# Disjoint segments in the STU's second products, and sums over states issued for two units together

## The chip, the cores and the metric

The kernel runs on one core of one Trainium2 chip. The metric is the device time of one execution in microseconds. All data is fp32.

## The reference

The input is four images of 48 × 48 tokens with 128 channels. Two layers are computed, one after the other, for each image.

The first is a state-space layer: projections, a 3 × 3 convolution, and a recurrence over the 2304 tokens in four directions k, for 256 channels with 16 states each:

```python
def step(h, inp):
    dt_l, u_l, B_l, C_l = inp
    dA = jnp.exp(dt_l[..., None] * A)
    h = h * dA + (dt_l * u_l)[..., None] * B_l[:, :, None, :]
    y = jnp.einsum('bkdn,bkn->bkd', h, C_l)
    return (h, y)
```

The second is an attention without projections, and after it an STU: a causal convolution of the sequence with 16 spectral filters, once plain (U_plus) and once with alternating signs (U_minus), and a product with a matrix for each filter, plus an autoregressive part over three shifted copies of the sequence:

There are four such STUs with their own matrices; the i-th reads only the first T, T/2, T/4 or T/8 tokens, and their results are added with four weights:

```python
out = jnp.einsum('btkd,k,kde->bte', U_plus, s, Mpp)
out = out + jnp.einsum('btkd,k,kde->bte', U_minus, s, Mpm)
...
for i, frac in enumerate((1, 2, 4, 8)):
    si = _stu(x[:, :T // frac], sigma, phi, M_u[i], M_phi_plus[i], M_phi_minus[i])
...
return jnp.sum(stacked * weights, axis=-1)
```

As the convolution is causal and the same for all four, a token's convolved rows are multiplied by one matrix: the weighted sum of the matrices of those STUs that reach the token. There are four such sums, with boundaries at tokens 288, 576 and 1152.

## The kernel before

**Stages.** For each image there is a scan stage (the recurrence), then an epilogue with the attention. The STU of an image is the filler of the next image's scan stage: `stu` is a generator that issues a few matmuls at a time, and `scans` calls it through `more(share)`, which pulls filler until the matmul columns issued so far (`done[0]`) reach the given share of all columns of the stage. In scan stage 0 the filler is `mixture`, which makes the mixed matrices G of the STU. The STU of the fourth image runs alone at the end. All loads and stores of these parts are issued by SP in program order; PE, VectorE (DVE), ScalarE (ACT) and GpSimd (POOL) each work through their own order, which is written out by hand.

**The scan.** A chunk is one direction and 384 tokens; a stage has 24 chunks. Of each chunk there are eight units (h, q), two halves of the channels by four groups of four states. Step s of `scans` deals with several units at once: `enter` multiplies the input for units s + 1 and s + 2 into a tile `s` (L457, five of eight units on DVE, three on POOL), `scan` runs unit s in four parts (L464 exponential on ACT, L467 scan on DVE), `times_c` multiplies unit s - 1 by C on POOL (L475, L476), `spread` makes the row B of unit s + 2 on PE (L448), and `sum_c` adds up the states of unit s - 2 on PE (L484): four matmuls with a 128 × 32 stationary matrix, each into its own 32 partitions of the bank `y`. After the fourth unit of a half, `add_y` adds the bank to the output on DVE (L490), one step later. The tiles `s` come from a pool of six buffers, the bank `y` from a pool of one.

**The STU.** Four tokens make a row, so that a sequence has 576 rows; `BLOCKS` cuts them into blocks (lo, hi, place, extra). For each block and each of 16 filters k, `conv` issues six groups of convolution matmuls (L990), with the filter's loaded windows `tt` (L960, four buffers) as moving operand; ACT and DVE take their results into U (L1004, L1016, L1019); and `project` multiplies U by the mixed matrices G (L1056) into the bank `p` (shown as `pr` in the profile) that is kept for the whole block. Once a block, `ar` adds the autoregressive products (L1046). In the first three blocks the sum of matrices changes after 72, 16 and 32 rows (rows 72, 144 and 288 of the sequence). There the kernel multiplies all rows by the matrix that holds after the boundary, and then the first `extra` rows once more by the difference to the one that holds before it:

```python
return ((w, 1), (extra, 0)) if extra else ((w, 0),)
```

So G and the autoregressive matrices are stored with six places: three differences and three accumulated mixtures. `mixture` makes them in two groups of matmuls (L847) for each filter and half, in two banks, and ACT copies each (L822).

Of the kernel before, what the change touches and what calls it, by code (L numbers as in the profile page):

```python
# [8 lines left out]
F32 = mybir.dt.float32  # L9
AF = mybir.ActivationFunctionType  # L10
ALU = mybir.AluOpType
# [4 lines left out]
P = 128  # L16
# [5 lines left out]
CS = 384  # L22
# [3 lines left out]
KF = 16  # L26
# [7 lines left out]
SLOT = 2 * (LF + 1)  # L34


BLOCKS = [(0, 128, 0, 72), (128, 256, 2, 16), (256, 384, 4, 32), (384, 512, 5, 0), (512, 576, 5, 0)]
SHIFT = 55.0


# [14 lines left out]
def hybrid_kernel(ctx: ExitStack, tc: tile.TileContext, a: dict, out: bass.AP):  # L55
# [80 lines left out]
    zs = res.tile([NH, P, L], F32, name="zd")  # L136
    td = res.tile([L, C], F32, name="td")
    ud = res.tile([P, 4, 1 + LF], F32, name="ud")
    gd = res.tile([KF, P, 2, 2 * NF - 2, C], F32, name="gd")
    mud = res.tile([P, 2 * NF - 2, 3, C], F32, name="mud")  # L140
    fd = res.tile([KF, 3, 2, LF + P], F32, name="fd")
    xdd = [[res.tile([P, CS], F32, name=f"xdd{k}_{c}") for c in range(L // CS)] for k in range(2)]

# [374 lines left out]
    def scans(b, chunks, preps, front, sp, back, work, work_cols):  # L518

        units = [Unit(ch, h, q) for ch in chunks for h, q in quads]  # L520
        total = len(chunks) * CHUNK_COLS + work_cols
        done = [0]

        def more(share):

            while done[0] < share * total:
                cols = next(work, None)
                if cols is None:
                    break
                done[0] += cols  # L530

        def enter(s):

            if s + 2 < len(units) and units[s + 2].pool:
                units[s + 2].enter(sp.s)
            if 0 <= s + 1 < len(units) and not units[s + 1].pool:
                units[s + 1].enter(sp.s)

        def spread(s):
            if s < len(units) and not units[s].pool:  # L540
                units[s].spread(back.psB)
                done[0] += CS

        def prepare(s):

            ci, j = divmod(s, len(quads))
            for c in range(ci + 1, ci + 4):
                if c < len(chunks) and 0 <= s - len(quads) * c + LEAD < STEPS:
                    done[0] += next(preps[c]) or 0

        def refill(s, i):

            if 0 <= s < len(units) and s // len(quads) + 1 < len(chunks):
                u, nxt = units[s], chunks[s // len(quads) + 1]
                if u.h == NH - 1:
                    nxt.fetch(i + u.q, front)

        pending = []
        dAs = [back.psa.tile([P, 512], F32, tag=f"dA{i}", name=f"dA{b}_{i}") for i in range(2)]
        for t in dAs:  # L560
            nc.vector.memset(t[:, 0:CS + 2:CS + 1], 0.0)
        spread(0)
        enter(-2)
        enter(-1)
        spread(1)
        for s in range(len(units) + 2):
            real = s < len(units)
            enter(s)
            prepare(s)
            if real:  # L570
                units[s].scan(0, dAs)
            more((s + 0.25) / len(units))
            if 1 <= s <= len(units):
                units[s - 1].times_c()
            if real:
                units[s].scan(1, dAs)
            if pending:
                pending.pop().add_y()
            prepare(s)
            more((s + 0.5) / len(units))  # L580
            spread(s + 2)
            if real:
                units[s].scan(2, dAs)
            more((s + 0.75) / len(units))
            prepare(s)
            if real:
                units[s].scan(3, dAs)
            refill(s - 3, Q4)
            if s + 1 < len(units) and units[s + 1].pool:
                refill(s + 1, 0)  # L590
            if s >= 2:
                units[s - 2].sum_c(back.psy)
                done[0] += CS
                if units[s - 2].q == Q4 - 1:
                    pending.append(units[s - 2])
            more((s + 1) / len(units))
        for u in pending:
            u.add_y()
        assert next(work, None) is None
# [141 lines left out]

    MIX_COLS = KF * 2 * 2 * (6 + 3) * C

    ws = wp.tile([P, KF, NF], F32, name="ws")

    def weights(one):
# [48 lines left out]
        quarter = one.tile([P, KF], F32, name="quarter")  # L797
        nc.vector.memset(quarter, 0.25)
        nc.gpsimd.tensor_tensor(sg, sg, quarter, ALU.pow)
        mum = one.tile([P, 2 * NF - 2, 3, C], F32, name="mum")  # L800
        nc.vector.tensor_scalar_mul(mum[:, 5], mu[:, 0], wts[:, 0:1])
        for i in range(1, NF):
            nc.vector.tensor_scalar_mul(mum[:, 6 - 2 * i], mu[:, i], wts[:, i:i + 1])
            if i < NF - 1:
                nc.vector.tensor_tensor(mum[:, 5 - 2 * i], mum[:, 7 - 2 * i], mum[:, 6 - 2 * i], ALU.add)
            yield
        nc.scalar.dma_start(mud, mum)
        for i in range(NF):
# [5 lines left out]
    def mixture(pool, ps):  # L814

        late = []
        banks = [0]

        def keep_(G, p, j, k, q):
            nc.scalar.copy(G[:, :, j], p)  # L822
            if j == 0:
                nc.sync.dma_start(gd[k, :, q], G.rearrange("p s j c -> p (s j) c"))

        for k in range(KF):
            M = [pool.two.tile([P, NF, C], F32, tag=f"M{j}", name=f"M{j}_{k}") for j in range(2)]
            for t, src in zip(M, ("M_phi_plus", "M_phi_minus")):
                nc.sync.dma_start(t, a[src][:, k].rearrange("i d e -> d i e"))

            W = pool.two.tile([P, 2, NF, P], F32, tag="W", name=f"W{k}")
            for i in range(NF):
                nc.scalar.activation(W[:, 0, i], ident, AF.Copy, scale=ws[:, k, i:i + 1])
                nc.scalar.activation(W[:, 1, i], nident, AF.Copy, scale=ws[:, k, i:i + 1])
            yield 0
            for q in range(2):
                G = pool.two.tile([P, 3, 2, C], F32, tag="Gm", name=f"Gm{k}_{q}")
                for j in (1, 0):
                    p = ps.psc.tile([P, 3, C], F32, tag=("c", "q0", "q1")[banks[0] % 3], name=f"G{k}_{q}_{j}")
                    banks[0] += 1  # L840
                    for i in range(NF):

                        n = NF - 1 - i if j else 1
                        if i == (NF - 1 if j else 0):
                            continue
                        for t in range(2):
                            nc.tensor.matmul(p[:, :n] if j else p[:, NF - 1 - i], W[:, q if t else 0, i],  # L847
                                             M[t][:, i].unsqueeze(1).to_broadcast([P, n, C]) if j else M[t][:, i],
                                             start=(t == 0 and (i == 0 or not j)),
                                             stop=(t == 1 and (i == NF - 2 or not j)))  # L850
                            yield n * C
                    if late:
                        keep_(*late.pop())
                    late.append((G, p, j, k, q))
        keep_(*late.pop())

    def begin_stu(b):
# [6 lines left out]
    def tail(b, J, T, po, pool, ps):  # L864
# [38 lines left out]
        for j in range(4):  # L903
# [5 lines left out]
        nc.sync.dma_start(ud[:, :, 1 + P * J:1 + P * J + k], uT.rearrange("c (j p) -> c j p", j=4))  # L909

    STU_COLS = sum(KF * 12 * sum(hi - max(lo, J * P) for J in range((hi + P - 1) // P))
                   + (2 * KF + 3) * 4 * (hi - lo + extra) + 4 * (hi - lo) for lo, hi, place, extra in BLOCKS)

    def stu(b, pool, ps):

# [116 lines left out]

        def parts(w, extra):

            return ((w, 1), (extra, 0)) if extra else ((w, 0),)

        def ar(n):

            (lo, hi, place, extra), k = items[n]
            w = hi - lo  # L1040
            p = ps.psp.tile([P, 512], F32, tag="p", name=f"pr{b}_{n}")
            now["p"] = p = p[:, :4 * w].rearrange("p (f r m) -> p f r m", f=2, r=2)
            for i, (v, x) in enumerate(parts(w, extra)):
                for j in range(3):
                    src = now["x"][:, 2 - j:6 - j].rearrange("p (r f) m -> p f r m", f=2)
                    nc.tensor.matmul(p[:, :, :, :v], now["mu"][:, x, j, :], src[:, :, :, :v],  # L1046
                                     start=(i == 0 and j == 0), stop=False)
            yield 3 * 4 * (w + extra)

        def project(n):  # L1050
            (lo, hi, place, extra), k = items[n]
            w = hi - lo
            p = now["p"].rearrange("p f r m -> p (f r) m")
            for q in range(2):
                for v, x in reversed(parts(w, extra)):
                    nc.tensor.matmul(p[:, :, :v], Gs[n][:, q, x, :], U[n][:, 4 * q:4 * q + 4, :v], start=False,  # L1056
                                     stop=(k == KF - 1 and q == 1 and v == w))
                yield 4 * (w + extra)
            if k == KF - 1:
                late.append(lambda: kept(n, now["p"], w))  # L1060

# [192 lines left out]
```

## Time and profile before

| | us |
|---|---|
| median of 3 runs (6332.32 to 6337.62) | 6336.3 |
| the profiled execution | 6347.6 |
| its span, first to last instruction | 6345.8 |
| PE busy | 5413.9 |
| DVE busy | 4482.4 |
| POOL busy | 3637.0 |
| ACT busy | 3050.9 |
| scan stage 0, first to last scan | 123.9 to 1136.7 |
| scan stages 1, 2 and 3 | 1439.0 to 2556.4, 2858.8 to 3976.8, 4278.8 to 5390.3 |
| the last STU alone | 5637 to 6345.8 |

Busy time is the time in which an engine has at least one instruction in work; for PE it is modelled. The profile comes from one execution, which took 11.3 us more than the median of the runs. In the profile each fp32 matmul appears as two records, so that counts of PE are twice those of the code. DMA share is the mean busy share of the core's 16 DMA engines.

### The profile page before, as it was taken

To read this page: it belongs to the slowest core of one execution; us is meant where nothing else is said; L and a number is where in the kernel's file an instruction comes from. 1 tells how busy PE (TensorE), PEld (TensorE's weight loads), DVE (VectorE), ACT (ScalarE), POOL (GpSimd) and SP (SyncE) were. 2 spreads that over 40 slices of the span, in tenths; PEclk is the share of its full clock that TensorE was granted. 3 is DMA by queue.
4 is the path that set the end of the run, shared out by engine and by line. 5 is a ranking of instruction groups with operands and counts; after the bars stand their busy time and mean duration, and the time that the engine had idled before them with its cause. 6 is when DMAs were issued, how large, how long until landed. Compare 5 with 4: busy or idle time off the path is not lost.

```text
span 6345.8 us, 76244 instructions
## 1 busy us (share of the span) xinstructions
PE 5413.9 (85%) x25032; PEld 3360.4 (53%) x25032; DVE 4482.4 (71%) x5562; ACT 3050.9 (48%) x6461; POOL 3637.0 (57%) x1825
## 2 busy tenths in 40 slices
PE   3665666788999998788999998789999998889999
PEld 1222222444555666534556667534555666557889
DVE  6998899458888997458889987458899987211000
ACT  2666666245555654245556654246566654222111
POOL 1888888306787886207778886207778877100000
PEclk6777787799999999899999999889999999899999
DMA  4656655127788888127788888127888887025446
GB/s 105 145 139 150 154 144 143 35 64 180 193 213 218 228 220 237 40 63 188 194 208 223 226 229 223 37 71 189 197 213 221 226 224 222 20 74 153 149 142 214
DMA packets 658251, 1033.57 MB, mean 163 GB/s; under 512 B 93856, under 2 KB 515872, under 8 KB 633120
## 3 DMA queue, kind: packets, MB, share of 16 engines
q1 hardware_dynamic: 652032, 1025.00, 62.7%
q10 hardware_dynamic: 5824, 3.69, 0.3%
q8 instruction: 200, 3.28, 0.2%
q14 instruction: 195, 1.60, 0.1%
HBM read 905.79 MB, written 122.56 MB: 162 GB/s over the span
## 4 chain that ended last, share of the span: by engine, by line
PE 50%; DMA 19%; DVE 18%; ACT 4%; SPq 3%; issue 3%; POOL 3%; DVEq 0%; ACTq 0%; POOLq 0%
PE cv L990 23%; DMA tt<-fd 8%; DVE s L467 7%; PE pr L1056 7%; DMA rep<-dtdud 6%; PE y L484 4%; DVE s L457 4%; PE s L726 3%; PE o L719 3%; DMA bc<-xdd 2%; PE B L448 2%; PE op L662 2%; DVE xc L266 2%; DMA G<-gd 2%; POOL s L476 2%
## 5 line engine op out<-in xcount | busy, mean ns | idle before, releaser
L467 DVE TENSOR_TENSOR_SCAN s<-dA,s 128x385 f32<-128x385 f32 x3072 | 2760.2, 942 | 382.8 <-ACT dA L464 379.6
L476 POOL TENSOR_TENSOR s<-s,bc 128x1536 f32<-128x1536 f32 x768 | 2439.0, 3177 | 200.7 <-DVE s L467 104.3
L464 ACT ACTIVATE dA<-rep,A 128x384 f32<-128x384 f32 x3072 | 1781.9, 585 | 1259.9 <-DVE s L467 1219.1
L990 PE MATMUL cv<-tt,u 128*128 128x256 f32 (+3 forms) x7680 | 1650.8, 354 | 129.2 <-DMA tt<-fd 65.5
L990 PEld LDWEIGHTS cv<-tt,u 128*128 128x128 f32 x7680 | 1271.9, 193 | 649.1 <-issue 303.9
L457 POOL TENSOR_TENSOR s<-rep,bc 128x1536 f32<-128x1536 f32 x288 | 994.0, 3451 | 92.9 <-DMA bc<-xdd 92.9
L457 DVE TENSOR_TENSOR s<-rep,B 128x1536 f32<-128x1536 f32 x480 | 832.8, 1735 | 83.3 <-PE B L448 54.1
L990 PE MATMUL cv<-tt,us 128*128 128x256 f32 (+3 forms) x3840 | 855.2, 352 | 37.2 <-DMA tt<-fd 31.3
L484 PE MATMUL y<-s,csum 128*32 128x384 f32 x6144 | 717.3, 542 | 115.1 <-DVE ya L490 78.8
L990 PEld LDWEIGHTS cv<-tt,us 128*128 128x128 f32 x3840 | 640.7, 192 | 231.5 <-issue 64.7
L1019 DVE TENSOR_TENSOR U<-cv,Q 128x256 f32<-128x256 f32 (+1 forms) x640 | 244.5, 382 | 705.5 <-PE cv L990 696.9
L1056 PE MATMUL pr<-U,G 128*128 128x512 f32 (+4 forms) x2048 | 693.2, 468 | 2.1 <-ACT U L1016 2.1
L448 PE MATMUL B<-xd,spread 128*128 128x384 f32 x960 | 440.1, 543 | 175.5 <-DVE s L457 166.7
L1016 ACT COPY U<-cv 128x256 f32<-128x256 f32 (+1 forms) x640 | 223.0, 349 | 700.9 <-PE cv L990 700.3
L475 POOL COPY carry<-s 128x4 f32<-128x4 f32 x640 | 120.7, 189 | 691.3 <-DVE s L467 660.0
L1056 PEld LDWEIGHTS pr<-U,G 128*128 128x128 f32 x2048 | 335.8, 190 | 193.6 <-issue 140.7
L1004 ACT COPY Q<-cv 128x256 f32<-128x256 f32 (+3 forms) x640 | 223.0, 349 | 385.2 <-PE cv L990 381.7
L726 PE MATMUL s<-xnT 128*128 128x512 f32 (+1 forms) x720 | 357.7, 582 | 42.6 <-ACT xnT L688 23.4
L728 ACT ACTIVATE e<-s,shift 128x512 f32<-128x512 f32 (+1 forms) x360 | 231.0, 644 | 314.1 <-PE s L726 313.5
L484 PEld LDWEIGHTS y<-s,csum 128*32 128x32 f32 x6144 | 127.1, 112 | 467.0 <-issue 314.0
L160 POOL TENSOR_TENSOR ln_vu<-ln_vu,mhalf 128x4 f32<-128x4 f32 (+1 forms) x20 | 26.8, 1340 | 601.9 <-DVE ln_vu L159 601.9
L719 PE MATMUL o<-e,xn 128*128 128x512 f32 (+1 forms) x720 | 343.2, 560 | 4.5 <-ACT e L728 4.5
(161 smaller groups left out, 3761.9 us busy)
## 6 DMA issues: line engine op xcount, KB each, us to landing
rep<-dtdud SPq DMA_DIRECT2D x768, 384.0 KB, 7.7
tt<-fd SPq DMA_DIRECT2D x192, 577.0 KB, 5.3
bc<-xdd SPq DMA_DIRECT2D x2304, 48.0 KB, 3.5
tt<-fd SPq DMA_DIRECT2D x192, 513.0 KB, 4.6
tt<-fd SPq DMA_DIRECT2D x192, 385.0 KB, 4.3
dtdud<-re SPq DMA_DIRECT2D x768, 96.0 KB, 2.3
G<-gd SPq DMA_DIRECT2D x192, 256.0 KB, 5.6
tt<-fd SPq DMA_DIRECT2D x64, 514.0 KB, 5.9
```

Of the source, the lines that this page charges most:

```text
L448: nc.tensor.matmul(self.bt[:, :CS], spread[:, self.ch.k // 2, self.q].rearrange("p c j -> p (c j)"), self.ch.xd, start=True, stop=True)
L457: eng.tensor_tensor(s, self.ch.rep[self.h][:, 1], bt.unsqueeze(1).to_broadcast([P, G4, CS]), ALU.mult)
L464: nc.scalar.activation(dA[:, 1:CS + 1], ch.rep[self.h][:, 0, g], AF.Exp, scale=A[:, ch.k, self.h * G4 + g, self.q:self.q + 1])
L467: nc.vector.tensor_tensor_scan(s, dA[:, CS + 1:0:-1] if ch.rev else dA[:, :CS + 1], s, 0.0, ALU.mult, ALU.add)
L476: nc.gpsimd.tensor_tensor(self.s, self.s, ch.bc[Q4 + self.q].unsqueeze(1).to_broadcast([P, G4, CS]), ALU.mult)
L484: nc.tensor.matmul(ch.y[g * DL:(g + 1) * DL, :CS], csum, self.s[:, g], start=(self.q == 0), stop=(self.q == Q4 - 1))
L719: nc.tensor.matmul(po[J][:, :w], xn[:, i], e[:, :w], start=(i == 0), stop=(i == NT - 1))
L726: nc.tensor.matmul(p[:, :w], xnT[:, i * P:(i + 1) * P], xnT[:, 512 * J:512 * J + w], start=True, stop=True)
L728: nc.scalar.activation(e[:, :w], p[:, :w], AF.Exp, bias=shift)
L990: nc.tensor.matmul(p2[:, :, at - first:], x, t[:, :, hi - 1 - at + J * P:end if end >= 0 else None:-1], start=(c < 2 and J == 0), stop=(J ...
L1019: nc.vector.tensor_tensor(dst, src, q, ALU.add)
L1056: nc.tensor.matmul(p[:, :, :v], Gs[n][:, q, x, :], U[n][:, 4 * q:4 * q + 4, :v], start=False, stop=(k == KF - 1 and q == 1 and v == w))
```

## The change

Two things change. In the STU, the rows before a boundary are multiplied by their own accumulated mixture and the rows after it by theirs: two disjoint segments of the bank in place of all rows and a correction. The mixture then has four places in place of six, made in one group of matmuls into one bank for each filter and half, with one copy and a smaller store. In the scan, the sums over states of units s - 3 and s - 2 are issued together at every second step, where before those of unit s - 2 were issued at each step. The counts of columns by which the filler is paced follow.

```diff
-BLOCKS = [(0, 128, 0, 72), (128, 256, 2, 16), (256, 384, 4, 32), (384, 512, 5, 0), (512, 576, 5, 0)]
+BLOCKS = [(0, 128, 0, 72), (128, 256, 1, 16), (256, 384, 2, 32), (384, 512, 3, 0), (512, 576, 3, 0)]
...
-    gd = res.tile([KF, P, 2, 2 * NF - 2, C], F32, name="gd")
-    mud = res.tile([P, 2 * NF - 2, 3, C], F32, name="mud")
+    gd = res.tile([KF, P, 2, NF, C], F32, name="gd")
+    mud = res.tile([P, NF, 3, C], F32, name="mud")
...
-            if s >= 2:
+            if s >= 2 and units[s - 2].q % 2:
+                units[s - 3].sum_c(back.psy)
                 units[s - 2].sum_c(back.psy)
-                done[0] += CS
+                done[0] += 2 * CS
                 if units[s - 2].q == Q4 - 1:
                     pending.append(units[s - 2])
...
-    MIX_COLS = KF * 2 * 2 * (6 + 3) * C
+    MIX_COLS = KF * 2 * NF * (NF + 1) * C
...
         for i in range(1, NF):
-            nc.vector.tensor_scalar_mul(mum[:, 6 - 2 * i], mu[:, i], wts[:, i:i + 1])
-            if i < NF - 1:
-                nc.vector.tensor_tensor(mum[:, 5 - 2 * i], mum[:, 7 - 2 * i], mum[:, 6 - 2 * i], ALU.add)
+            nc.vector.tensor_scalar_mul(mum[:, NF - 1 - i], mu[:, i], wts[:, i:i + 1])
+            nc.vector.tensor_tensor(mum[:, NF - 1 - i], mum[:, NF - 1 - i], mum[:, NF - i], ALU.add)
...
-        def keep_(G, p, j, k, q):
-            nc.scalar.copy(G[:, :, j], p)
-            if j == 0:
-                nc.sync.dma_start(gd[k, :, q], G.rearrange("p s j c -> p (s j) c"))
+        def keep_(p, k, q):
+            G = pool.two.tile([P, NF, C], F32, tag="Gm", name=f"Gm{k}_{q}")
+            nc.scalar.copy(G, p)
+            nc.sync.dma_start(gd[k, :, q], G)
...
-                for j in (1, 0):
-                    p = ps.psc.tile([P, 3, C], F32, tag=("c", "q0", "q1")[banks[0] % 3], name=f"G{k}_{q}_{j}")
...
+                p = ps.psc.tile([P, NF, C], F32, tag=("c", "q0", "q1")[banks[0] % 3], name=f"G{k}_{q}")
+                banks[0] += 1
+                for i in range(NF):
+
+                    n = NF - i
+                    for t in range(2):
+                        nc.tensor.matmul(p[:, :n], W[:, q if t else 0, i],
+                                         M[t][:, i].unsqueeze(1).to_broadcast([P, n, C]),
+                                         start=(t == 0 and i == 0), stop=(t == 1 and i == NF - 1))
+                        yield n * C
...
-                   + (2 * KF + 3) * 4 * (hi - lo + extra) + 4 * (hi - lo) for lo, hi, place, extra in BLOCKS)
+                   + (2 * KF + 3) * 4 * (hi - lo) + 4 * (hi - lo) for lo, hi, place, extra in BLOCKS)
...
-            return ((w, 1), (extra, 0)) if extra else ((w, 0),)
+            return ((0, extra, 0), (extra, w, 1)) if extra else ((0, w, 0),)
...
-            for i, (v, x) in enumerate(parts(w, extra)):
+            for v0, v1, x in parts(w, extra):
                 for j in range(3):
                     src = now["x"][:, 2 - j:6 - j].rearrange("p (r f) m -> p f r m", f=2)
-                    nc.tensor.matmul(p[:, :, :, :v], now["mu"][:, x, j, :], src[:, :, :, :v],
-                                     start=(i == 0 and j == 0), stop=False)
-            yield 3 * 4 * (w + extra)
+                    nc.tensor.matmul(p[:, :, :, v0:v1], now["mu"][:, x, j, :], src[:, :, :, v0:v1],
+                                     start=(j == 0 and v0 == 0), stop=False)
+            yield 3 * 4 * w
...
             for q in range(2):
-                for v, x in reversed(parts(w, extra)):
-                    nc.tensor.matmul(p[:, :, :v], Gs[n][:, q, x, :], U[n][:, 4 * q:4 * q + 4, :v], start=False,
-                                     stop=(k == KF - 1 and q == 1 and v == w))
-                yield 4 * (w + extra)
+                for v0, v1, x in parts(w, extra):
+                    nc.tensor.matmul(p[:, :, v0:v1], Gs[n][:, q, x, :], U[n][:, 4 * q:4 * q + 4, v0:v1], start=False,
+                                     stop=(k == KF - 1 and q == 1 and v1 == w))
+                yield 4 * w
```

More of the change, by code (lines that the diff above doesn't have):

```diff
@@ L799, in weights @@
         nc.gpsimd.tensor_tensor(sg, sg, quarter, ALU.pow)
-        mum = one.tile([P, 2 * NF - 2, 3, C], F32, name="mum")
-        nc.vector.tensor_scalar_mul(mum[:, 5], mu[:, 0], wts[:, 0:1])
+        mum = one.tile([P, NF, 3, C], F32, name="mum")
+        nc.vector.tensor_scalar_mul(mum[:, NF - 1], mu[:, 0], wts[:, 0:1])
         for i in range(1, NF):
-            nc.vector.tensor_scalar_mul(mum[:, 6 - 2 * i], mu[:, i], wts[:, i:i + 1])
-            if i < NF - 1:
-                nc.vector.tensor_tensor(mum[:, 5 - 2 * i], mum[:, 7 - 2 * i], mum[:, 6 - 2 * i], ALU.add)
+            nc.vector.tensor_scalar_mul(mum[:, NF - 1 - i], mu[:, i], wts[:, i:i + 1])
+            nc.vector.tensor_tensor(mum[:, NF - 1 - i], mum[:, NF - 1 - i], mum[:, NF - i], ALU.add)
             yield
@@ L836, in mixture @@
             for q in range(2):
-                G = pool.two.tile([P, 3, 2, C], F32, tag="Gm", name=f"Gm{k}_{q}")
-                for j in (1, 0):
-                    p = ps.psc.tile([P, 3, C], F32, tag=("c", "q0", "q1")[banks[0] % 3], name=f"G{k}_{q}_{j}")
[L840 to L854, printed above, removed]
+                p = ps.psc.tile([P, NF, C], F32, tag=("c", "q0", "q1")[banks[0] % 3], name=f"G{k}_{q}")
[7 more added lines that the diff above has]
+                        yield n * C
+                if late:
+                    keep_(*late.pop())
+                late.append((p, k, q))
         keep_(*late.pop())
```

## The prediction

> **What bounds the kernel now.** I read the slices of the page first. They fall into four scan stages, an attention stage after each, and a last stage in which the STU of the fourth image runs alone. Then I cut the span into windows. The first row below is scan stage 0 (with the weight mixture as filler), the next three are thirds of scan stage 2 (with the STU of image 1 as filler), the last is the lone STU. Columns: microseconds, busy time with instruction counts of the named engines, granted clock, DMA share, GB/s.
>
> ```profile
> core 0: us, PE busy (x) PEld busy (x) DVE busy (x) ACT busy (x) POOL busy (x), PEclk, DMA share, GB/s
> 149.00:1090.00 941.00, 580.78 (x2533) 234.89 (x2532) 855.86 (x917) 583.41 (x1195) 812.98 (x399) 0.78 0.61 147
> 2860.00:3310.00 450.00, 416.94 (x1850) 240.50 (x1851) 385.14 (x457) 264.05 (x580) 341.46 (x168) 0.97 0.80 196
> 3310.00:3760.00 450.00, 438.99 (x2143) 278.16 (x2143) 419.00 (x483) 273.91 (x578) 380.69 (x183) 1.00 0.88 224
> 3760.00:3965.00 205.00, 178.19 (x1293) 140.51 (x1292) 159.71 (x190) 98.17 (x232) 144.85 (x70) 0.94 0.83 230
> 5637.00:6345.80 708.80, 698.82 (x3460) 568.28 (x3460) 67.09 (x165) 115.14 (x325) 0.00 (x0) 0.99 0.54 161
> ```
>
> The lone STU is PE and nothing else (699 of 709 us). Stage 0 is the scan's DVE (91%), and PE has 360 us to spare. Stages 1 to 3 look alike: PE leads at 93% to 98%, DVE follows at 86% to 93%, DMA at 0.80 to 0.88. The chain of waits, asked for a stretch of the middle third and then of the last third, says which holds where:
>
> ```profile
> by line: PE cv L990 61.1%; PE y L484 14.4%; PE pr L1056 10.7%; PE B L448 6.9%; PE dt L386 3.4%; issue 1.9%; DVE s L467 1.8%; DVE s L457 0.1%
> ...
> by line: DMA tt<-fd 36.3%; PE cv L990 35.9%; PE y L484 6.8%; DVE s L467 4.4%; PE B L448 3.7%; DVE s L457 3.5%; PE pr L1056 3.0%; PE dt L386 1.4%; DMA bc<-xdd 1.3%; DVE re L414 0.8%; issue 0.8%; PE pr L1046 0.7%; DVE U L1019 0.4%; PE ot L107
> ```
>
> From 3560 to 3660 us it is a PE chain; from 3770 to 3960 us (the 64-row block) the filter loads take over a third. For the prices I read PE's timeline. Each fp32 matmul is two records, so the sum of one unit over states, four matmuls, is "x8".
>
> ```profile
> 3309.46 0.60 PE L990 MATMUL cv<-tt,us 128*128 128x258 f32 x2
> 3309.99 0.85 PE L484 MATMUL y<-s,csum 128*32 128x384 f32 x8
> 3310.77 1.13 PE L990 MATMUL cv<-tt,us 128*128 128x258 f32 x4
> 3311.74 1.24 PE L1056 MATMUL pr<-U,G 128*128 128x128 f32 x4
> ...
> 3318.99 0.81 PE L448 MATMUL B<-xd,spread 128*128 128x384 f32 x2
> 3319.63 0.59 PE L990 MATMUL cv<-tt,u 128*128 128x256 f32 x2
> ...
> 5663.85 2.85 PE L1056 MATMUL pr<-U,G 128*128 128x288 f32 x8
> 5666.53 1.47 PE L990 MATMUL cv<-tt,u 128*128 128x256 f32 x6
> ```
>
> Durations of PE overlap, so starts are what counts. From start to start a 256-column record takes 0.216 us, 384 columns 0.32 (the B row: 0.64 for two), 288 columns 0.242, 512 columns 0.429, so 0.83 ns a column. The pr row checks it: 4 × 0.429 + 4 × 0.242 = 2.68 = 5666.53 - 5663.85. Around y the rule breaks. Two cv records take 0.53 instead of 0.43 before it, y takes 0.78 instead of 0.65 (two rounds of four concurrent column groups), the four cv records after it 0.97 instead of 0.87. The medians over all y groups of stages 1 to 3 are 0.093 + 0.129 + 0.107 = **0.33 us lost for each y group**.
>
> **What the skill says.** TensorEngine Tiling (Array Packing), Key Properties: changing the tiling mode drains TensorE, and tiles of one mode run independently. The trace agrees: the 0.33 us stand where 128*128 and 128*32 meet, the four y records of a round start 7 ns apart, and where two units follow each other at the end of stage 1 (2552.24 us) their rounds start at 0, 0.35, 0.67, 0.99 us, with nothing lost between units. PSUM — Partial Sum Buffer, Specifications, says that a non-contiguous access pattern slows matmuls much, which would hit the 56-column segments that the change brings. The trace disagrees: the existing segments of 4 × 72 columns take 0.242 us, what 288 contiguous columns would. DMA: Bandwidth & Descriptors, Issuing engines are not separate DMA queues: all share 16 engines; the last third, with 230 GB/s and the tt chain, fits that.
>
> **The change, part by part.** *Second products (L1056).* Per half q a block with a boundary had one full-width product and one of 4 × extra columns; now it has 4 × extra and 4 × (w - extra). The count stays, two matmuls of two records. Block 0 loses 288 columns (429 to 189 ns a record), block 1 64 (429 to 375), block 2 128 (429 to 323): 2 × (240 + 54 + 106) = 800 ns per half, × 2 halves × 16 filters = 25.6 us per image. *Autoregressive products (L1046)*, once a block, 3 matmuls of 2 records: 6 × 0.40 = 2.4 us. Together **28 us of PE per image**. G and mue loads keep their sizes; their weight loads stay hidden under records of 189 ns or more, and where a 64-column record is shorter, it was so before.
>
> *Sums of two units together (L484).* Of 192 y groups a stage 96 lose their neighbours: 96 × 0.33 = **31.6 us of PE per scan stage**. Moved are the four matmuls of each even unit, by one step, past that step's filler, B and dt matmuls on PE; no DMA and no instruction of SP, POOL, ACT or DVE moves with them. The filler takes their columns, so B comes no later. The bank y is asked for again a step later than now, so PE's wait for DVE ya (78.8 us in all, 62.7 in stage 0) goes. Added is a hold: an even unit's s buffer comes free a step later. Six buffers go round; I followed the reuse. Odd units are already summed two steps before their buffer is entered again, even ones three; now all have two. That slack is enough today: the only engine shown waiting for y to release s is POOL, 0.2 us, once. I price the hold at 0; what covers it is that step of slack, and without it see rival 3.
>
> *Mixture (stage 0) and preparation.* 768 records become 512, columns per filter and half go from 18 to 20 × 128, which costs PE at most 20 us out of its 360 idle. ACT does 32 copies of about 0.58 us (the 512-column o copy) in place of 64 of 0.47: 11 us less. 32 stores shrink from 384 to 256 KB, one from 1152 to 768. One DVE addition is new, 0.56 us, under the first loads.
>
> **What arrives at the end.** *Lone STU:* PE is 100% busy from 5655 to 6208 us, where blocks 0 to 2 run, and DMA at 0.5 there can follow block 0's 18% shorter filters: **-28**. *Stages 1 to 3:* PE work falls by 60 us, or 0.31 us a step, of 192 steps. I go by chunks of 8 steps (2.5 us of PE each), timed from scan to scan. Chunks 0 to 9 take about 48 us; PE (93%) is followed by DVE (86%) and tt loads: I take 2.0 each, 20. Chunks 10 to 19 take 42 to 44 us with DVE at 93% to 96%, and its floor is 1.5 to 3 us below: 0.8 each, 8. Chunks 20 to 23 take 50 to 58 us and wait for tt; bytes stay: 1. That is **29 a stage, 87**. It is the chosen term: from below 0 (all lost to DVE and DMA), from above 60. *Stage 0:* DVE's own idle for B, POOL and issue is 28 us, part of it because PE sat on ya: **-7** (0 to 20). Sum -122. The profiled execution took 6347.6 us (span 6345.8), so it would take 6226; the median of the three runs is 11.3 below the profiled one, so **6214 us**. A measurement of this kernel tells about 0.2% (13 us) from nothing.
>
> **Rivals.** *1. Only the lone STU gains (15%).* For: in the stages DVE is at 86% to 93%, each faster step asks DMA for the same bytes in less time, and a stalled PE falls to a lower clock (0.94 in the last third against 1.00). Against: the PE-only chain at 3560. Then 28 + 15: 6293. *2. The stages follow PE in full (8%).* For: the PE chain; against: DVE would stand at 97% and more. 3 × 60 + 28 + 15: 6113. *3. Slower: the hold binds (5%).* 24 chunks × 4 even units × 4 images = 384 entries into s lose a step of slack. If POOL's or DVE's entry waits for the pair, the scan behind it waits too. Gain and loss meet at 122 / 384 = 0.32 us per entry; at 0.5 us it costs 192 and the kernel ends at 6214 + 192 = 6406. Against it: odd units live with the same slack, and no wait shows. *4. The columns don't pay (3%)*: if a short segment costs a full-width record, the products give nothing, and of the stage gain only the drains' part stays, 87 × 31.6 / 60 + 7 = 53: 6283. The 72-column segments speak against it.
>
> **How the numbers follow.** Likeliest, 69%: 6214, own range 6170 to 6270. The range 6165 to 6295 takes in rivals 1 and 4 and leaves out rivals 2 and 3 and thin tails, under 2 in 10. Faster 0.95 (likeliest, 1, 2 and 4), same 0.01 (rival 3 where its loss just meets the gain), slower 0.04 (the rest of rival 3).
>
> **What would show it.** Right: in the lone STU a block-0 filter takes 4.3 us instead of 5.3 and the stage about 681 us; y shows x16, with 1.44 us from its start to the next row's; no PE wait for DVE ya; PE's busy time down by some 200 us; DVE share up in stages 1 to 3, the last third hardly shorter. Wrong: the 224-column records not near 0.19 us, POOL L457 or DVE L457 waiting for PE y, or stages 1 to 3 as long as now with more tt waits.

## The result: 0.1% to 0.3%, and where the forecast gain stayed out

The changed kernel takes **6329.4 us** (median of 4 runs, 6325.5 to 6333.2) against 6336.6 us before on the same chip (4 runs): ratio 0.999, 95% interval 0.9973 to 1.0007. Measured again with 12 runs on another chip, where the kernel before takes 6349.4 us, the ratio is 0.9975 (0.9966 to 0.9984), so there is a gain, of a quarter of a per cent. Forecast were 6214 us (6165 to 6295). The kernel before takes 6337 to 6353 us on the chips used here, so every ratio below is against the kernel before on the same chip.

The profiled execution took 6333.2 us (span 6331.5), before 6347.6 (6345.8). From the first scan to the last scan of each stage, in us:

| | stage 0 | stages 1 to 3 in sum | last scan to the end | span |
|---|---|---|---|---|
| before | 1012.8 | 3346.9 | 955.5 | 6345.8 |
| after | 1023.2 | 3349.2 | 928.7 | 6331.5 |
| forecast difference | -7 | -87 | -28 | |
| measured difference | +10.4 | +2.3 | -26.8 | -14.3 |

The lone STU gave what was forecast. The scan stages gave nothing. Stage times here and below come from one profiled execution of each kernel, and stages 1 to 3 of one kernel differ among themselves by up to 13 us, so a few us in one stage mean little.

First the windows of the kernel after, at the places of those shown of before (scan stage 0, three thirds of scan stage 2, the lone STU); columns are the length, busy time with counts for each engine, granted clock, DMA share and GB/s.

```profile
core 0: us, PE busy (x) PEld busy (x) DVE busy (x) ACT busy (x) POOL busy (x), PEclk, DMA share, GB/s
149.00:1100.00 951.00, 562.19 (x2284) 222.58 (x2283) 856.69 (x917) 575.70 (x1165) 813.48 (x399) 0.77 0.59 141
2876.00:3326.00 450.00, 402.04 (x1914) 259.88 (x1915) 387.83 (x463) 265.39 (x587) 341.73 (x170) 0.97 0.84 202
3326.00:3776.00 450.00, 418.81 (x2103) 280.10 (x2102) 414.83 (x478) 271.37 (x573) 380.88 (x182) 0.98 0.85 219
3776.00:3981.00 205.00, 172.20 (x1284) 141.94 (x1284) 161.45 (x192) 98.47 (x232) 145.12 (x70) 0.93 0.82 228
5650.00:6331.50 681.50, 672.09 (x3460) 568.11 (x3460) 67.15 (x165) 115.32 (x325) 0.00 (x0) 0.99 0.56 168
```

In the three windows of stage 2 PE is busy 993 us where it was 1034, and nothing else rose in its place: DVE's busy time is the same within 1%, and so is the DMA share. PE's work went and left idle time. The chain of waits in the stretch that was a pure PE chain before (100 us from the same distance after the stage's start, then the last third) shows what stood right behind PE:

```profile
by line: DVE s L467 25.8%; DMA tt<-fd 14.2%; DVE s L457 10.2%; DMA rep<-dtdud 9.7%; PE cv L985 9.1%; issue 5.5%; DMA bc<-xdd 5.3%; DVE re L414 2.5%; ACT L464 2.4%; ACT dA L464 2.3%; PE dt L386 1.8%; PE pr L1051 1.7%; PE y L484 1.7%; DVE U L
by line: PE cv L985 32.5%; DMA tt<-fd 26.0%; PE y L484 7.3%; DMA rep<-dtdud 5.1%; PE B L448 4.3%; DMA bc<-xdd 3.8%; SPq L403 3.5%; PE pr L1051 3.2%; DVE s L467 2.8%; issue 2.7%; SPq L435 1.9%; ACT dA L464 1.8%; DVE s L457 0.9%; DVE re L414 
```

PE's convolutions fell from 61% to 9% of the first stretch; the scan on DVE and three kinds of load took their place. The five chunks that begin there take no less time: 215.9 us, before 214.4. The prices of the single operations, in PE's timeline of after (start, us, row):

```profile
3620.13 1.50 PE L484 MATMUL y<-s,csum 128*32 128x384 f32 x16
3621.56 1.57 PE L985 MATMUL cv<-tt,us 128*128 128x258 f32 x6
...
5678.34 1.89 PE L1051 MATMUL pr<-U,G 128*128 128x288 f32 x8
5680.07 1.47 PE L985 MATMUL cv<-tt,u 128*128 128x256 f32 x6
```

The pair of sums takes 1.43 us from start to start (1.44 forecast), and a block-0 product 1.73 us for eight records, 4 × 0.242 + 4 × 0.189. So the prices stand. What PE's time turned into shows in its waits, some of the longest (total us, times, longest us); before, then after:

```profile
PE B L448 <- DVE s L457: 166.7, 73, 7.0
PE cv L990 <- DMA tt<-fd: 96.8, 45, 7.6
PE dt L386 <- DVE s L457: 88.1, 59, 3.6
PE y L484 <- DVE ya L490: 78.8, 32, 5.8
PE G L847 <- DMA M<-in_M_phi_plus: 75.2, 12, 17.0
```

```profile
PE B L448 <- DVE s L457: 233.2, 95, 7.4
PE cv L985 <- DMA tt<-fd: 142.3, 57, 7.6
PE dt L386 <- DVE s L457: 131.3, 63, 7.2
PE G L843 <- DMA M<-in_M_phi_plus: 107.0, 14, 17.3
PE y L484 <- DVE ya L490: 11.3, 2, 5.7
```

The wait for `ya` is nearly gone, as forecast. The waits for the loads of tt and M grew by 77 us, and those for DVE's entries into `s` (L457) by 110 us. In stages 1 to 3 alone PE's wait for tt grew from 88 to 135 us, for G from nothing to 22, and for L457 before B and dt from 36 to 82: part of PE's time went to late loads and part to DVE. DVE's wait for the bank y, the other side of the pair, grew as well, before and after:

```profile
DVE ya L490 <- PE y L484: 27.0, 14, 5.3
```

```profile
DVE ya L490 <- PE y L484: 79.0, 36, 6.7
```

PE's lower mean clock (0.910, before 0.921) does not show in its records: in stages 1 to 3 the median time from the start of a 256-column convolution record to the next record is 0.216 us in both kernels.

### The profile page after: what moved, and what is told of

Its sections match the earlier page's. It is cut to its first block, busy times and chain, and to the rows that moved or that the text cites. A ratio compares the mean times of both kernels' runs of the same rounds, so it can differ in the third digit from the quotient of the medians.

```text
span 6331.5 us, 75588 instructions
## 1 busy us (share of the span) xinstructions
PE 5248.3 (83%) x24776; PEld 3413.4 (54%) x24776; DVE 4479.7 (71%) x5563; ACT 3036.4 (48%) x6429; POOL 3638.1 (57%) x1825
## 4 chain that ended last, share of the span: by engine, by line
PE 45%; DVE 21%; DMA 19%; ACT 5%; issue 4%; SPq 3%; POOL 2%; DVEq 0%; ACTq 0%; POOLq 0%
PE cv L985 20%; DVE s L467 9%; DMA tt<-fd 6%; PE pr L1051 5%; DMA rep<-dtdud 5%; DVE s L457 5%; PE s L727 4%; DMA G<-gd 4%; PE y L484 4%; DMA bc<-xdd 3%; PE o L720 3%; PE op L663 2%; PE B L448 2%; DVE xc L266 2%; DVE re L414 2%
## 5 line engine op out<-in xcount | busy, mean ns | idle before, releaser
L476 POOL TENSOR_TENSOR s<-s,bc 128x1536 f32<-128x1536 f32 x768 | 2440.0, 3179 | 193.9 <-DVE s L467 108.3
L985 PE MATMUL cv<-tt,u 128*128 128x256 f32 (+3 forms) x7680 | 1627.2, 354 | 195.6 <-DMA tt<-fd 116.9
L985 PEld LDWEIGHTS cv<-tt,u 128*128 128x128 f32 x7680 | 1285.4, 194 | 612.1 <-issue 236.3
L457 POOL TENSOR_TENSOR s<-rep,bc 128x1536 f32<-128x1536 f32 x288 | 993.3, 3449 | 109.8 <-DMA bc<-xdd 96.2
L457 DVE TENSOR_TENSOR s<-rep,B 128x1536 f32<-128x1536 f32 x480 | 834.0, 1737 | 71.3 <-PE B L448 40.2
L484 PE MATMUL y<-s,csum 128*32 128x384 f32 x6144 | 655.0, 548 | 39.9 <-POOL s L476 28.6
L1051 PE MATMUL pr<-U,G 128*128 128x288 f32 (+7 forms) x2048 | 593.2, 423 | 23.8 <-DMA G<-gd 22.0
L484 PEld LDWEIGHTS y<-s,csum 128*32 128x32 f32 x6144 | 171.5, 117 | 403.3 <-issue 309.6
L448 PEld LDWEIGHTS B<-xd,spread 128*128 128x128 f32 x960 | 178.8, 205 | 376.1 <-DVE s L457 290.2
L160 POOL TENSOR_TENSOR ln_vu<-ln_vu,mhalf 128x4 f32<-128x4 f32 (+1 forms) x20 | 26.8, 1342 | 601.8 <-DVE ln_vu L159 601.8
```

The lines of the kernel that those rows point to most:

```text
L448: nc.tensor.matmul(self.bt[:, :CS], spread[:, self.ch.k // 2, self.q].rearrange("p c j -> p (c j)"), self.ch.xd, start=True, stop=True)
L457: eng.tensor_tensor(s, self.ch.rep[self.h][:, 1], bt.unsqueeze(1).to_broadcast([P, G4, CS]), ALU.mult)
L476: nc.gpsimd.tensor_tensor(self.s, self.s, ch.bc[Q4 + self.q].unsqueeze(1).to_broadcast([P, G4, CS]), ALU.mult)
L484: nc.tensor.matmul(ch.y[g * DL:(g + 1) * DL, :CS], csum, self.s[:, g], start=(self.q == 0), stop=(self.q == Q4 - 1))
L985: nc.tensor.matmul(p2[:, :, at - first:], x, t[:, :, hi - 1 - at + J * P:end if end >= 0 else None:-1], start=(c < 2 and J == 0), stop=(J ...
L1051: nc.tensor.matmul(p[:, :, v0:v1], Gs[n][:, q, x, :], U[n][:, 4 * q:4 * q + 4, v0:v1], start=False, stop=(k == KF - 1 and q == 1 and v1 == w))
```

## The experiments

All kernels are variants of before or after; times are medians, the stages are those of the table above. Of each edit the main lines are shown.

**Each part alone.** `e1_segments` is after with `sum_c` issued unit by unit as before; `e2_pairs` is before with the paired sums.

```diff
-            if s >= 2 and units[s - 2].q % 2:
-                units[s - 3].sum_c(back.psy)
+            if s >= 2:
                 units[s - 2].sum_c(back.psy)
-                done[0] += 2 * CS
+                done[0] += CS
```

> The segments alone, sums unit by unit as before. Theory A (the freed PE time is real in both parts, but the pairs bring new waits: DVE on y for add_y 79 us instead of 27, POOL on y 13.6 us instead of 0.2): the segments keep their own gain, 27 us in the lone STU and some 12 us in each of stages 1 to 3, so about 6275. Theory B (stages 1 to 3 are paced by loads and by DVE, whatever PE saves): only the lone STU's 27 us, 6300 to 6310, and block 0 (chunks 0 and 1) some 9 us longer in each stage.

Measured 6320.0 us, ratio 0.9951 (0.9936 to 0.9965): lone part -22, stages 1 to 3 -15 in sum, stage 0 +7.

> The pairs alone, products as before. Theory A: as long as before or longer, 6336 to 6370, with the waits of DVE and POOL for y and the 10 us more in stage 0. Theory B: stages 1 to 3 unchanged within 5 us each, stage 0 unchanged, 6325 to 6340.

Measured 6315.2 us, ratio 0.9943 (0.9928 to 0.9957): stages 1 to 3 -32 in sum, stage 0 -2, lone part +2. Neither theory had expected the pairs to gain this much.

> The changed kernel once more, as the yardstick beside the others on one chip: 0.996 to 0.9995 of the kernel before, stages 1 to 3 at 1110 to 1124 us, stage 0 at 1018 to 1026.

The kernel after, unedited: 6334.7 us, ratio 0.9975 (0.9966 to 0.9984). Each part alone is faster than both together: 33 and 38 us alone, 15 us in one kernel. Half the relief of PE still buys time in stages 1 to 3, all of it buys none. If PE runs into things that are late, repairing them must bring the gain back; the next runs try that one by one.

**The late load of G.** In the first two chunks of stages 1 to 3, which lie inside block 0, the kernel after is slower: 112.6, 109.3 and 109.3 us against 101.6, 100.8 and 100.3. Its waits there, in the first 114 us of stage 2:

```profile
PEld pr L1051 <- DMA G<-gd: 7.5, 2, 4.1
PE pr L1051 <- DMA G<-gd: 6.5, 2, 3.4
```

`e4_early_G` gives G a third buffer and asks for it one filter earlier (room comes from Q, which drops to one buffer).

```diff
-                Gs[n] = pool.two.tile([P, 2, 2, C], F32, tag="G", name=f"G{b}_{n}")
+                Gs[n] = pool.three.tile([P, 2, 2, C], F32, tag="G", name=f"G{b}_{n}")
...
+        fetch_G(0)
...
-                    fetch_G(n)
+                    fetch_G(n + 1)
```

> The changed kernel with three buffers for G and its load issued one filter earlier (Q with one buffer makes the room). If the longer chunks 0 and 1 of stages 1 to 3 (+9 to +11 us each) are the late G of block 0, PE's 22 us of waits for G go and 20 to 30 us come back, 6300 to 6310. If it is the queue of all loads, the wait moves to tt or rep and the time stays within 10 us of 6329.

Measured 6307.7 us, ratio 0.9930 (0.9913 to 0.9946). The first two chunks are back at 99.4, 99.0 and 99.4 us, and PE no longer waits for G. Stages 1 to 3 fall by 26 us against after. So PE had outrun a load that was in time before. It takes both parts to do so: with the segments alone (e1) PE waits half as long for G, and the two chunks take 102.7 us in the mean, before 100.9.

**The late load of M.** `e5_early_M` loads the mixture's M for filter k + 1 before it works on filter k.

```diff
...
+        load_M(0)
         for k in range(KF):
-            M = [pool.two.tile([P, NF, C], F32, tag=f"M{j}", name=f"M{j}_{k}") for j in range(2)]
-            for t, src in zip(M, ("M_phi_plus", "M_phi_minus")):
-                nc.sync.dma_start(t, a[src][:, k].rearrange("i d e -> d i e"))
+            load_M(k + 1)
+            M = Ms.pop(k)
```

> The changed kernel with the mixture's matrices M loaded one filter ahead. PE waits 107 us for M in the changed kernel and 75 before. If those waits hold B and dt back and so make stage 0 longer (1023 us against 1013), the wait falls under 30 us and stage 0 comes to 1000 to 1013, stages 1 to 3 unchanged: 6310 to 6320. If stage 0 hangs on DVE and its exponentials alone, it stays at 1018 to 1026.

Measured 6305.1 us, ratio 0.9932 (0.9916 to 0.9948). Stage 0 falls from 1017 us in e6 on the same chip to 980.9, below the 1000 to 1013 expected, and what is left of the wait is the first load:

```profile
PE G L851 <- DMA M<-in_M_phi_plus: 17.4, 1, 17.4
```

**The wait of `add_y`.** With pairs, twice as many sums are issued just ahead of the step in which DVE adds the bank. `e3_late_add` moves the addition behind the step's fourth scan instead of its second.

```diff
-            if pending:
-                pending.pop().add_y()
             prepare(s)
...
                 units[s].scan(3, dAs)
+            if pending:
+                pending.pop().add_y()
             refill(s - 3, Q4)
```

> The changed kernel with add_y half a step later (after the unit's fourth scan instead of its second), so that the pair has time to end before DVE asks for it. Theory A: DVE's wait for PE y falls from 79 us to under 30 and about 30 to 50 us come back, 6280 to 6300. Theory B: the wait goes and the time stays, 6320 to 6335.

Measured 6323.3 us, ratio 0.9956 (0.9938 to 0.9974), an interval that overlaps that of e6. DVE's wait fell from 79 to 25.8 us and stage 0 by 22 us, but stages 1 to 3 gained nothing (3354.9 in sum): there this wait was not what counted.

**Both loads in time, on both kernels.** `e10_after_early` is after with the edits of e4 and e5, `e11_before_early` before with the same, `e12_early_late_add` is e10 with that of e3.

> The changed kernel with both late loads repaired: M one filter ahead, G one filter ahead with three buffers (Q with one). If the two gains of 30 and 27 us are separate, 6270 to 6285 on a chip where the kernel before takes 6350: ratio 0.988 to 0.990.

> The kernel before with the same two repairs. G waits were 0 there and M waits 75 us, so stage 0 gains some 25 to 33 us, stages 1 to 3 nothing: 6315 to 6325, ratio 0.995 to 0.996. The difference to the changed kernel with the repairs is then what the change is worth where its loads come in time: 27 us of the lone STU and some 5 to 8 us a stage, 40 to 55 us. If it is under 25 us, the repairs are worth the same to both and late loads are not where the change lost.

> The changed kernel with both repairs and add_y half a step later. If DVE's wait for y still costs stage 0 its 16 to 20 us, 15 to 25 us below the one without it: 6250 to 6268. If stage 0's gain from the later add was the wait for M in another place, within 8 us of it.

Measured e10 6268.0 us, 0.9869 (0.9854 to 0.9885); e11 6326.0 us, 0.9957 (0.9942 to 0.9971); e12 6266.6 us, 0.9868 (0.9853 to 0.9883). With these loads in time the change is worth 58 us, where it was worth 7 and 15 as given, and near the 70 of the two parts alone. In the profiled spans it is 47 (e10's is the slowest of its four runs): the lone part 27, stage 0 6 (981.3 against 987.0), stages 1 to 3 14 in sum. e10 and e12 are the fastest kernels here that leave nothing out. The late addition takes 10 us off stage 0 in e12, but stages 1 to 3 are 8 us longer in that profile, and the whole is the same.

**Half of the filter loads.** Stages 1 to 3 still give only 14 us of the 87 forecast. `e7_half_after` and `e8_half_before` use the windows `tt` of each even filter again for the odd one, so that the odd filters' own windows are left out.

```diff
-        order = [(n, cs) for n in range(len(items)) for cs in slots(n)]
+        order = [(n, cs) for n in range(0, len(items), 2) for cs in slots(n)]
...
-                    tts[i, x] = t[:, 2 * (x - cs[0]):2 * (x - cs[0]) + 2]
+                    tts[i, x] = tts[i + 1, x] = t[:, 2 * (x - cs[0]):2 * (x - cs[0]) + 2]
```

> The changed kernel, in which each odd filter reuses the windows of the even filter before it, so that half of the tt loads are left out (and the odd filters' own windows with them). Theory B1 (loads take what PE frees): PE's wait for tt, 142 us, falls under 60, and stages 1 to 3 go to 1040 to 1075 us each, near PE's 60 us of saving below 1118; with the kernel before under the same relief staying 35 us or more a stage above it. Theory B2 (DVE and its waits for ACT hold the stages): under 25 us a stage gained, and the same level for both kernels.

> The kernel before with the same half of the tt loads left out. Theory B1: PE bounds it then, as PE's 1033 us of work a stage and its few waits say: 1085 to 1110 a stage, and the difference to the changed kernel under the same relief is 35 to 60 us a stage. Theory B2: the two kernels come within 10 us of each other in stages 1 to 3.

Measured 6207.1 us, 0.9779 (0.9764 to 0.9793), and 6255.9 us, 0.9854 (0.9838 to 0.9870). Both kernels gain, by 93 to 116 us in stages 1 to 3, so these loads do hold them; but they lie only 20 us apart there in all, though PE's busy time differs by 43 to 48 us in each of the three stages. Neither theory fits in whole: the first asked for 35 to 60 us between them in each stage, the second, which had them within 10 us of each other, for a gain of less than 25 us a stage.

**DVE relieved as well.** `e9_half_no_add` is e7 without the addition on DVE.

```diff
         def add_y(self):
             ch = self.ch
-            v = in_order(yaccs[ch.b][self.h], ch.k, ch.lo, CS)
-            nc.vector.tensor_tensor(v, v, ch.y[:, :CS].rearrange("p (r w) -> p r w", w=v.shape[2]), ALU.add)
+            return
```

> The changed kernel with half of the tt loads left out and with add_y left out as well (the scan's sums are not added to the output): 48 DVE instructions of 0.67 us a stage, 32 us of DVE, are gone, and with them DVE's waits for y. If DVE is what holds stages 1 to 3 once the loads are out of the way, they go from 1078 to 1040 to 1055 us each and stage 0 from 1018 to 985 to 1000, 6075 to 6110. If PE or the exponentials on ACT hold them, they stay within 10 us of 1078, above 6170.

Measured 6171.3 us, 0.9718 (0.9704 to 0.9733). Against e7, stage 0 fell by 25 us of the 32 taken, stages 1 to 3 by only 7 each in the mean (2 to 10): the theory that DVE's work alone bounds them is wrong.

**ACT's waits.** ACT takes PE's results in program order, with exponentials of the scan behind them; in the middle 1000 us of stage 2 it stands 117 us (after) and 112 us (before) for these banks. In `e13_free_copies_after` and `e14_free_copies_before` (e10 and e11 otherwise) the same copies read a tile in SBUF, and the STU's convolutions are left out of its result. The edit also spares PE its own short waits for these copies.

```diff
-                nc.scalar.copy(Q[g], p[:, :2 * nw])
+                nc.scalar.copy(Q[g], u[:, 0].rearrange("p j c -> p (j c)")[:, :2 * nw])
...
-                nc.scalar.copy(dst, src)
+                nc.scalar.copy(dst, u[:, 0].rearrange("p j c -> p (j c)")[:, :2 * w].rearrange("p (e m) -> p e m", e=2))
```

> The kernel after with M and G loaded one filter ahead (as in e10), and ACT's copies Q and U of the STU take their numbers from a tile in SBUF instead of PE's bank: same count, same shapes, but ACT no longer waits for PE's convolutions (the STU's output is not the reference's). Theory 1, ACT hands PE's delays on to the scan: ACT stood some 120 to 165 us a stage waiting for these banks, with the next exponentials behind it in its order, and DVE waits about 80 us a stage for exponentials. Then stages 1 to 3 lose 20 us or more each against e10 (1107 to 1118 us) and the kernel takes 6210 us or less. Theory 2, the loads and PE's own order hold the stages: ACT's waits only move, stages 1 to 3 stay within 8 us of e10's, and the kernel takes 6250 to 6275 us.

> The kernel before with the same two early loads (as in e11) and the same copies from SBUF as in e13. e11 took 6326 us. If ACT is what couples PE to the scan (theory 1), the kernel before is then the more held by PE, which has 60 us a stage more work, and stands 90 us or more above e13. If ACT doesn't matter (theory 2) the distance stays at the 58 us between e11 and e10, two thirds of it in the lone STU.

Measured 6231.1 us, 0.9812 (0.9796 to 0.9828), and 6266.0 us, 0.9870 (0.9852 to 0.9887). DVE's wait for exponentials, 2880 to 3880 us, in e10 and then in e13:

```profile
DVE s L467 <- ACT dA L464: 64.2, 63, 3.0
```

```profile
DVE s L467 <- ACT dA L464: 25.3, 30, 1.3
```

The coupling is real and costs 16 us a stage in either kernel (3332.9 to 3284.5 and 3347.2 to 3298.7 in sum). It is not what swallowed the change: the two still lie only 14 us apart in stages 1 to 3, and 35 us in medians, where the first theory asked for 90. The 16 us a stage lie between the two theories.

**Hardly any filter loads.** `e15_once_after` and `e16_once_before` (e10 and e11 otherwise) load `tt` once a block and use it for all sixteen filters.

```diff
-        order = [(n, cs) for n in range(len(items)) for cs in slots(n)]
+        order = [(n, cs) for n in range(0, len(items), KF) for cs in slots(n)]
...
-                    tts[i, x] = t[:, 2 * (x - cs[0]):2 * (x - cs[0]) + 2]
+                    for f in range(KF):
+                        tts[i + f, x] = t[:, 2 * (x - cs[0]):2 * (x - cs[0]) + 2]
```

> The kernel after with M and G early (as in e10), and the filter windows tt loaded only for the first filter of each block and used again for the other fifteen (the other filters' convolutions are left wrong). Theory 2, loads hold the stages: with hardly any tt load the stages 1 to 3 fall well under the 1075 to 1083 us that half the loads gave (e7), to 1030 to 1050 us each, and the kernel to 6060 to 6110 us. Theory 3, PE and DVE both near full and coupled in order: they stay at 1065 to 1080 us, and the kernel at 6140 to 6180 us.

> The kernel before with M and G early (as in e11), and the windows tt loaded only for the first filter of each block. If the loads were what swallowed the change's gain in stages 1 to 3 (theory 2), then without them PE is what is left, and this kernel stands some 60 us a stage above e15, 150 us or more in all. If PE and DVE share the bound (theory 3), stages 1 to 3 differ from e15's by 5 to 15 us each, and the kernels by 60 to 90 us.

Measured 6118.3 us, 0.9633 (0.9619 to 0.9648), and 6218.2 us, 0.9795 (0.9780 to 0.9809). They lie 100 us apart in medians and 70 us in stages 1 to 3: 23 a stage, where PE's busy time differs by 49 to 52. That is between the theories, 60 a stage for the loads and 5 to 15 for the shared bound. By chunks, mean of the three stages, in us:

| chunks | 0 to 1 | 2 to 9 | 10 to 14 | 15 to 19 | 20 to 23 |
|---|---|---|---|---|---|
| forecast | -4 | -16 | -4 | -4 | -1 |
| after - before, as given | +9.5 | -8.7 | +0.5 | +0.6 | -1.3 |
| e15 - e16 | -2.4 | -7.6 | -2.3 | +0.5 | -11.7 |

The 23 come near the 29 forecast by luck: half of them lie in chunks 20 to 23, where 1 was forecast.

Chunks 15 to 19 take 209.5 us in all three stages of e16 and in one of e15's to the tenth, and 209.5 and 210.0 in the mean of e8 and e7. The windows of these chunks in stage 2, of e15 and then of e16:

```profile
3452.00:3660.00 208.00, 197.40 (x1029) 134.49 (x1029) 198.13 (x229) 129.98 (x273) 181.75 (x86) 0.99 0.62 143
```

```profile
3498.00:3706.00 208.00, 207.61 (x1040) 134.60 (x1041) 198.99 (x230) 130.69 (x276) 181.53 (x87) 1.00 0.62 144
```

PE stands at 100% in e16 and at 95% in e15, DVE at 95% to 96% in both, DMA at 0.62. PE's 10 us are gone and the stretch is as long: here the loads of tt are not what held it. In e15's window PE waits nearly as long for DVE's entries instead:

```profile
PE B L448 <- DVE s L457: 5.7, 4, 2.4
PE dt L386 <- DVE s L457: 3.2, 3, 1.1
```

In chunks 2 to 9 the loads of tt hold little either: the kernel after takes 369.9 us there as given and 368.4 without them. With ACT's copies freed (e13 and e14) both kernels take 364.6 us there in the mean, so that the gain of the change in these chunks seems to have come by way of ACT's waits for PE.

The same five chunks 15 to 19 take 202.2 us in e10's stage 0, where no STU runs, and DVE's additions into U, 403 ns each, come on top; that fits a scan whose own order on DVE sets the pace in chunks 15 to 19, but e9 took 6.5 us of DVE out of these chunks (ten additions of 0.65) and got 1.1 to 3.4.

## Why the prediction was wrong

- **Prices: right.** The segments cost what 0.83 ns a column says, the pair loses no drain between its units. PE's busy time fell by 166 us of the 200 forecast (5413.9 to 5248.3): by 41 in the windows of stage 2 where 60 were forecast. The runs don't say where the rest is.
- **Lone STU, -28: right**, -26.8. A block-0 filter went from 5.30 to 4.41 us in the median where 5.3 to 4.3 was forecast; eight of the sixteen filters have a new wait of PE's weight load for ACT's copy Q, 3.1 us in all.
- **The hold of s, priced 0: nearly right.** POOL L457 waits 13.6 us for PE's y in all, and did not before (the 0.2 us that the prediction names were at L476). What the prediction missed is the other end of the pair: DVE waits 52 us more for the bank y. e3 and e12 show that this costs stage 0 10 to 22 us and stages 1 to 3 nothing.
- **Mixture priced 0, stage 0 at -7: wrong** (+10). The cover named was PE's idle time of 360 us, but 75 us of that was itself a wait for M, which has no lead. The wait grew to 107 us, and e5, e10 and e11 show what it costs: with M early the change gains 6 us in stage 0. That this is about the 7 forecast is partly luck, as the late bank y takes 10 us from the same stage (e12). The wait for `ya`, of which the prediction counts 62.7 us in stage 0, lay there in full.
- **Stages 1 to 3, -87: the step that failed** (+2). It turned PE's 2.5 us a chunk into 2.0, 0.8 and about 0.2 us of kernel time, by how busy PE and DVE are in each range of chunks, and put the lead of the loads that a faster PE asks for sooner at nothing. What came in its place is late loads of G and longer waits for tt and for DVE's entries. For chunks 0 and 1 (-4 forecast) the loads of G came late, +9.5; e4 shows it. For chunks 2 to 9 it was half right (-8.7 of -16). For chunks 10 to 19 (-8 forecast) nothing came: a faster PE does not reach the DVE headroom of 1.5 to 3 us a chunk that the step named, as e15 against e16 shows for chunks 15 to 19. For chunks 20 to 23 the forecast of about nothing was right for the reason named, the tt loads: without them the change gives 12 us there (e15 against e16). The shares that the step starts from, PE at 93% to 98% and DVE at 86% to 93%, are those of the first two thirds; the last third has 87% and 78%.
- **Rivals.** Nearest was the first, that only the lone STU gains (6293; the 15 us that it and rival 2 add to the 28 are not worked out). Its cause, the same bytes asked for in less time, holds for chunks 20 to 23, as e15 against e16 shows, and not for chunks 15 to 19. A sign of being wrong that the prediction itself named, stages 1 to 3 as long as now with more tt waits, is what came.

**What stays open.** In chunks 2 to 19, with M and G early and nearly all tt loads out of the way, PE's busy time is 37 us a stage less in e15 than in e16, and that gives 9. ACT's waits, DVE's additions and the loads of tt were each taken away; none is the bound by itself. Which of the scan's own waits (POOL's carry, the loads of `rep` and `bc`, the order of DVE) sets the pace there wasn't tried. Nor is it shown why e1 and e2 keep half of a gain that both together lose, beyond the loads of G and M.

## What to carry to other kernels

Before freed time of the leading engine is counted, list each load that it will ask for sooner and how far ahead that load is issued: here PE outran a two-buffer load once both parts of the change were in, and part of the idle time named as cover was a wait for a load without lead. Where two engines stand near 90% or above and wait for each other in order, an engine's share of the span is no exchange rate: 37 to 52 us of PE's busy time less in a stage bought 0, 5, 7 and 23 us, in the mean of the stages, depending on the loads beside it. A change that gives next to nothing is worth trying again after its late loads are moved: 7 to 15 us became 58.

## What the runs showed of the hardware

An fp32 output in four separate segments of a bank costs no more than a contiguous one: 4 segments of 56 columns took 0.189 us a record, 4 of 72 took 0.242, and the 0.83 ns a column of contiguous records make 0.186 and 0.239. The Trainium skill's PSUM — Partial Sum Buffer, Specifications, calls a non-contiguous pattern a significant slowdown, and no run here shows one for segments of this length. Two rounds more of 128*32 matmuls in one group add 0.65 us and no further drain. PE's mean granted clock was 0.921 before, 0.910 after with less work and more waits, and 0.921 again without most tt loads (e15); the start-to-start time of a 256-column record stayed at 0.216 us.
